# A hyperbolic transformer block on one core: q, k, v kept in PSUM, biases as one-partition products, row scalars of eight tiles

## The chip, the core and the metric

The kernel runs on one core of one Trainium2 chip. The metric is the device time of one execution in microseconds (us); a lower figure is better. Times are medians of several runs on the same chip. Each profile comes from one execution, recorded by the hardware profiler: its span runs from the first instruction to the last, and its own time is a little longer. Engine names: PE is TensorE (matmul), PEld its weight loads, DVE is VectorE, ACT is ScalarE, POOL is GpSimd, SP is SyncE, which issues the DMAs here.

## The reference

The block works on x of 128 x 64 x 256 (8192 tokens of width D = 256, 16 heads of 16) with a condition vector of 256 per sequence. All is in 32-bit floats. Vectors live in the Poincare ball: `logmap0` and `expmap0` go to the tangent space and back and only change a row's length; `mobius_add` is the ball's addition.

```
ada = t_emb @ w_ada + b_ada                     # six vectors of 256 per sequence
xn = layer_norm(logmap0(x))
xm = expmap0(xn * (1 + sc_msa) + sh_msa)
q, k, v = (_to_heads(plin(xm, w, b)) for each)  # plin: expmap0(logmap0(x) @ w + b)
attn = softmax(qt @ kt / sqrt(16)) ; out_h = expmap0(attn @ vt)   # qt, kt, vt = logmap0
x = mobius_add(x, expmap0(g_msa * logmap0(plin(_from_heads(out_h), w_o, b_o))))
xn = layer_norm(logmap0(x)) ; xm = expmap0(xn * (1 + sc_mlp) + sh_mlp)
ff = plin(plin(xm, w_f1, b_f1), w_f2, b_f2)
result = input + mobius_add(x, expmap0(g_mlp * logmap0(ff)))
```

`logmap0(expmap0(u))` is u times a factor: 1, or the largest allowed length over the length of u. Many steps therefore reduce to one clip factor per row, or per row and head.

## The kernel before

**Tiles.** 128 tokens (two sequences of 64) make a tile, 64 in all; two tiles are a pair, four are a quad. A group G is 4 tiles, so there are 16 groups of one quad each. Each group goes through `attention` and then `mlp`.

**Attention of a quad.** `modulated` (line 791) scales and shifts x into y (ACT or DVE), multiplies and adds the condition rows (DVE, POOL), squares (ACT) and finds the clip factor fy per row. `transposed` (809) turns y over on PE into a wide PSUM tile and copies it to yT. Then `attention_pair` (832) runs twice: products with wqkv into a wide PSUM tile qk per tile; one DVE instruction per tile (line 843) forms u = qk * fy + bias in SBUF, which frees the PSUM; ACT squares u; DVE sums the squares per head (hs) and over all heads; a reciprocal root (Ln and Exp on ACT, three steps on DVE) gives the factor g per head; POOL scales q and k in place (859), DVE scales v into ve (861). Then come transposes of q and k (tq), scores (sc, products on 32 x 64 pieces of the array), Exp, products with ve (av, on 64 x 64 pieces), division, transposes (tz), the product with wo and its bias (wp), and `gated` (820), with products and sums of squares. At the group's end `mobius_scalars` (624) works out two scalars per row from these sums in 31 DVE instructions on 128 x 4 or 128 x 8 numbers, and a and b are applied.

**MLP of a quad.** `norm_scalars` (583) gives the layer norm's scalars in 32 DVE instructions on 128 x 4 numbers, then `modulated` and a scaling of y by fy (974), `transposed`, products with two 256 x 256 matrices that were made at the start from w_f1 and w_f2 (hm for the row's length, hw for the value), the clip factor fh, `gated`, `mobius_scalars`, and the output. For the first layer norm the same scalars are computed in a few batches of many tiles (`statistics`).

**Biases.** The q, k, v bias is broadcast over 128 partitions and added by the DVE instruction of line 843. wo's and the MLP's biases are products over 128 partitions with `first`, a matrix whose first row is ones and the rest zeros.

**PSUM.** The eight banks are two wide tiles of two banks (tag `dbl`: qk, tq, two sc at once, av, tp) and four narrow ones of one bank (`bank`: tz, wp, hm, hw and the fillers).

**Order.** The class `Plan` collects all operations with their dependences and an estimated cost each. `run` (150) walks through time: whenever an engine is free it takes the ready operation with the smallest key that finds its buffers free. The key is the group's number; an MLP's key is its group's plus LAG = 3. An operation with several possible engines goes to whichever is free first. A DVE operation that may not run beside POOL is held back. A PE group (`pl.group`) is issued without anything in between. When PE finds nothing, it gets a filler: a 128 x 128 product of the identity (`warm`, 1021). The order found is then issued as it stands, each engine working through its own queue in that order; all DMAs go through SP's queue.

Of the kernel before, what the change touches and what calls it, by code (L numbers as in the profile page):

```python
# [23 lines left out]
SCL = 2.0**-16  # L24
# [31 lines left out]
class Plan:  # L56
# [367 lines left out]
    def mm(self, out, lhsT, rhs, start, stop):  # L424
        n, k = self._n(rhs), lhsT.shape[0]
        occ = 2 * max(n / 1200.0 + 0.002, 0.11) if k == 128 else 0.031 if k == 64 else 0.0356
# [20 lines left out]
def kernel(  # L447
# [44 lines left out]
    G = 4  # L492
    NG = NT // G
    R = _beta(HD / 2, 0.5) / _beta(D / 2, 0.5)
    assert S == 64 and D == 256 and NT % G == 0 and G % 4 == 0
# [19 lines left out]
    def bank(name):  # L515
        return pl.tile(ps, [P, 512], "bank", name, 4, space="psum")

    def dbl(name):
        return pl.tile(ps, [P, 1024], "dbl", name, 2, space="psum")
# [18 lines left out]

    ves = [C([P, 2, H, HD + 1], f"ve{k}") for k in range(2)]
    for v in ves:  # L540
        nc.vector.memset(v, R)
# [7 lines left out]
    def load_x(g):  # L549
        t = T([P, G, D], "x", f"x{g}", 2)  # L550
        for h in range(G // 4):
            i0 = g * G + 4 * h
            pl.dma(t[:, 4 * h : 4 * h + 4, :], x_t[:, i0 : i0 + 4, :], 512 * KB, rows.last if g else None)
        xs[g] = t


    def rsqrt_core(o, ss, tag, room=0):

        shape = list(ss.shape)
        room = [P, max(shape[1], room)] if len(shape) == 2 else shape  # L560
        e = small(room, tag + "e", 2)[:, : shape[1]]
        pl.act(e, ss, AF.Ln)
        pl.act(e, e, AF.Exp, scale=-0.5)
        t = small(room, tag + "t", 2)[:, : shape[1]]
# [4 lines left out]
    def rsqrt_scaled(ss, tag):  # L569

        shape = list(ss.shape)
        m = small(shape, tag + "m", 2)
        pl.ts(m, ss, EPS2, SCL, ALU.max, ALU.mult)
        o = small(shape, tag + "o", 2)
        rsqrt_core(o, m, tag)
        return o

    def clip_factor(o, ss, tag):

        r = rsqrt_scaled(ss, tag)  # L580
        pl.ts(o, r, A * RSCL, 1.0, ALU.mult, ALU.min)

# [41 lines left out]
    def mobius_scalars(x2, wp, xpd, tag):  # L624
# [3 lines left out]
        def sc(k, bufs=1):  # L628
            return small([P, G], tag + k, bufs)

        p2 = wp[:, 1, :]
        r = rsqrt_scaled(wp, tag + "r")
# [41 lines left out]
    for n, w in ((0, 512), (1, 1024)):  # L674
        wada.append([T([P, w], "yTm" if n else "hT", f"wada{n}{c}", 2 if n else NJ + 1) for c in range(2)])
    for n in range(3):
        bada.append(T([P, 512], "hT", f"bada{n}", NJ + 1))
        ada.append(T([P, 512], "hT", f"ada{n}", NJ + 1))
# [8 lines left out]
    bo = C([P, D], "bo")  # L687
# [408 lines left out]
```

## Time and profile before

| | |
|---|---|
| median of 3 runs | 939.68 us (939.16 to 941.25) |
| profiled execution, own time | 937.61 us |
| its span | 935.4 us |
| PE / DVE / ACT / POOL busy | 86% / 87% / 56% / 18% |
| mean granted TensorE clock | 0.931 |
| instructions in the profile | 25226 |
| moved by DMA | 92.07 MB, mean 98 GB/s |

In a row of a group, the names are out<-in, then partitions x elements, the count after x, then busy us in all and the mean duration of one in ns, then the idle time of the engine just before them and what ended it. Buffer names end in a for attention and m for the MLP. A 32-bit product appears as two MATMUL instructions. In a timeline row the first two numbers are start and duration in us. Durations of successive instructions of one engine overlap a little, so a total of durations is more than the engine's occupied time.

### The profile page before, as it was taken

How to read it: one execution, taken by the hardware profiler on the slowest of the kernel's cores; microseconds unless marked ns; L12 is line 12 of the kernel's file. 1: busy time of each engine (PE TensorE's matmuls, PEld its weight loads, DVE VectorE, ACT ScalarE, POOL GpSimd, SP SyncE). 2: the span in 40 equal slices, each digit the busy share in tenths (PEclk: the TensorE clock that was granted, in tenths of full speed). 3: DMA queues.
4: the chain of work that ended last, by engine and by line, in shares of the span. 5: the costliest groups of instructions: out<-in, count | busy, mean ns of one | idle time of the engine just before them, and what ended most of it. 6: DMA issues, size and time to landing. Idle time of an engine off the chain costs nothing.

```text
span 935.4 us, 25226 instructions
## 1 busy us (share of the span) xinstructions
PE 802.7 (86%) x9356; PEld 631.3 (67%) x9356; DVE 817.8 (87%) x3521; ACT 523.4 (56%) x1575; POOL 170.7 (18%) x158
## 2 busy tenths in 40 slices
PE   6989897889888797988879988979898799988786
PEld 4555666758676675867667757858685686667676
DVE  5767979998998999898989998897988889997987
ACT  2342455756565655566557666556555566755542
POOL 0020213112130321202032212121130312221110
PEclk9899888999999899999989998898989799997999
DMA  6793333233332242224225223332232233211222
GB/s 197 232 263 114 109 103 100 80 97 101 114 86 75 77 114 72 75 78 122 81 70 134 92 60 103 90 113 81 80 114 80 58 94 89 80 59 47 68 68 68
DMA packets 77131, 92.07 MB, mean 98 GB/s; under 512 B 7120, under 2 KB 59088, under 8 KB 77008
## 3 DMA queue, kind: packets, MB, share of 16 engines
q1 hardware_dynamic: 77008, 90.47, 33.2%
q8 instruction: 73, 1.20, 0.5%
q14 instruction: 50, 0.41, 0.1%
HBM read 81.27 MB, written 9.18 MB: 97 GB/s over the span
## 4 chain that ended last, share of the span: by engine, by line
DVE 23%; PE 21%; ACT 10%; issue 4%; POOL 1%; DVEq 0%; POOLq 0%; ACTq 0%
PE wpa L427 3%; PE hmm L427 3%; PE ava L427 3%; PE wt L1023 2%; DVE ua L382 2%; PE hwm L427 2%; PE sca L427 2%; DVE hs L395 2%; PE tqa L431 1%; PE qkva L427 1%; DVE bx L382 1%; ACT j2m L420 1%; ACT j2a L420 1%; PE tpm L431 1%; ACT qxa L420 1%
## 5 line engine op out<-in xcount | busy, mean ns | idle before, releaser
L427 PE MATMUL qkva<-wqkv,yTa 128*128 128x512 f32 (+1 forms) x512 | 178.3, 499 | 15.6 <-DVE ua L382 5.3
L427 PEld LDWEIGHTS qkva<-wqkv,yTa 128*128 128x128 f32 x512 | 96.7, 194 | 90.8 <-issue 61.0
L1023 PE MATMUL wt<-ident 128*128 128x128 f32 x828 | 124.8, 305 | 1.8 <-DVE fm L382 1.4
L375 POOL TENSOR_TENSOR ua<-ua,g 128x512 f32<-128x512 f32 x64 | 73.7, 1171 | 281.0 <-DVE g L382 81.0
L1023 PEld LDWEIGHTS wt<-ident 128*128 128x128 f32 x828 | 115.9, 217 | 9.0 <-issue 5.8
L420 ACT ACTIVATE usqa<-ua 128x768 f32<-128x768 f32 x64 | 53.9, 842 | 67.8 <-DVE ua L382 38.7
L375 POOL TENSOR_TENSOR ym<-ym,mdm 128x512 f32<-128x512 f32 x32 | 42.9, 1347 | 214.8 <-DVE rho L382 61.4
L427 PEld LDWEIGHTS ava<-ve,pta 64*64 64x64 f32 x4096 | 70.2, 146 | 13.9 <-ACT pta L420 8.3
L427 PE MATMUL ava<-ve,pta 64*64 64x17 f32 x4096 | 74.5, 215 | 4.5 <-ACT pta L420 4.3
L427 PE MATMUL hmm<-wm,yTm 128*128 128x256 f32 x256 | 70.7, 397 | 5.2 <-ACT yTm L406 3.2
L420 ACT ACTIVATE pta<-sca 128x1024 f32<-128x1024 f32 x64 | 61.9, 1017 | 21.3 <-PE sca L427 21.3
L420 ACT ACTIVATE qxa<-tqa,par 128x512 f32<-128x512 f32 x64 | 43.6, 685 | 49.8 <-PE tqa L431 37.1
L382 DVE SCALAR_TENSOR_TENSOR ua<-qkva,fya,bqkv 128x768 f32<-128x768 f32 x64 | 64.7, 1011 | 7.1 <-PE qkva L427 6.6
L427 PE MATMUL wpa<-wo,zTa 128*128 128x256 f32 x256 | 70.1, 398 | 0.0
L431 PE MATMUL tqa<-ident,ua 128*128 128x128 f32 x256 | 44.6, 320 | 28.9 <-POOL ua L375 28.9
L427 PE MATMUL hwm<-wm,yTm 128*128 128x256 f32 x256 | 66.1, 381 | 0.0
L395 DVE TENSOR_REDUCE hs<-usqa 128x48 f32<-128x768 f32 x64 | 60.6, 947 | 3.7 <-ACT usqa L420 3.6
L427 PE MATMUL sca<-qxa,kTa 32*64 32x128 f32 x2048 | 46.3, 307 | 19.5 <-ACT qxa L420 13.0
L427 PEld LDWEIGHTS hmm<-wm,yTm 128*128 128x128 f32 x256 | 48.0, 196 | 15.9 <-ACT yTm L406 5.7
L375 POOL TENSOR_TENSOR ya<-ya,mda 128x512 f32<-128x512 f32 x30 | 39.9, 1335 | 100.6 <-DVE ya L372 28.5
L431 PEld LDWEIGHTS tqa<-ident,ua 128*128 128x128 f32 x256 | 33.4, 160 | 35.1 <-POOL ua L375 33.7
L427 PEld LDWEIGHTS sca<-qxa,kTa 32*64 32x64 f32 x2048 | 36.2, 147 | 29.7 <-ACT qxa L420 19.1
(257 smaller groups left out, 1808.9 us busy)
## 6 DMA issues: line engine op xcount, KB each, us to landing
mda<-ada_d SPq DMA_DIRECT2D x64, 256.0 KB, 4.1
mdm<-ada_d SPq DMA_DIRECT2D x64, 256.0 KB, 4.0
x<-in_x_dram SPq DMA_DIRECT2D x16, 512.0 KB, 3.7
xr<-in_x_dram SPq DMA_DIRECT2D x32, 256.0 KB, 2.8
gaa<-ada_d SPq DMA_DIRECT2D x64, 128.0 KB, 2.9
gmm<-ada_d SPq DMA_DIRECT2D x64, 128.0 KB, 3.0
out_dram<-p SPq DMA_DIRECT2D x16, 512.0 KB, 3.4
xp<-in_x_dram SPq DMA_DIRECT2D x30, 256.0 KB, 2.8
```

The source lines that it names most:

```text
L375: fn2 = lambda: self.nc.gpsimd.tensor_tensor(out, a, b, op)
L382: fn = lambda: self.nc.vector.scalar_tensor_tensor(out, a, s, b, op0, op1, **({} if accum is None else {"accum_out": accum}))
L395: fn = lambda: self.nc.vector.tensor_reduce(out, a, AX.X, ALU.add)
L420: fn = lambda: self.nc.scalar.activation(out, a, func, scale=scale, **kw)
L427: fn = lambda: self.nc.tensor.matmul(out, lhsT=lhsT, rhs=rhs, start=start, stop=stop)
L431: self.add([("PE", lambda: self.nc.tensor.transpose(out, a, ident), 0.112, 0.2, False)], [a, ident], [out])
L1023: nc.tensor.matmul(wt[:, 0:P], lhsT=ident, rhs=ident, start=True, stop=True)
```

## The change

- **q, k, v in PSUM.** qk is now one wide tile for q and k of both tiles of a pair, and vv one narrow tile for both v. They stay unscaled; squares are taken from PSUM by ACT (1024 and 512 elements at once), the factors are found, and DVE writes u = qk * g and ve = vv * g from PSUM. The row's clip factor f cancels in the factor per head where that clips, and else enters through a lower limit (`lim`, from `rq`), so fy isn't applied to q, k, v. POOL no longer takes part. A constant GC left out of g goes into the scale of the Exp and the constant column of ve.
- **Biases by one-partition products.** Since the rows are not scaled by f, the bias has to be added as bias / f: `clip_factor` also gives inv = 1/f, `transposed` turns it over on PE (four transposes of a broadcast column into a narrow tile) and copies it to rT, and a product of one partition of rT and one of the bias adds it in PSUM. The partitions are 0, 32 and 64 (for the MLP 0, 32, 64 and 96). wo's bias becomes one product of 512 columns per pair.
- **MLP.** y is no longer scaled by fy; the sums and fh are multiplied by it instead. hm and hw of a quad are each one wide PSUM tile.
- **Row scalars of 8 tiles.** The groups are quad 0, then (1, 2), (3, 4) to (13, 14), then 15: nine in all. `mobius_scalars` and the MLP's `norm_scalars` run once per group, on up to 8 columns.
- **PSUM and SBUF.** Three wide tiles and two narrow ones. y has two buffers in place of one, x is loaded in four buffers of a quad, and start-up data shares other tags. LAG is 3.5, the batches of statistics are cut at other quads, and the planner has a cost for one-partition products.

```diff
     def bank(name):
-        return pl.tile(ps, [P, 512], "bank", name, 4, space="psum")
+        return pl.tile(ps, [P, 512], "bank", name, 2, space="psum")
     def dbl(name):
-        return pl.tile(ps, [P, 1024], "dbl", name, 2, space="psum")
+        return pl.tile(ps, [P, 1024], "dbl", name, 3, space="psum")
...
+    GROUPS = [[0]] + [[q, q + 1] for q in range(1, NQ - 1, 2)] + [[NQ - 1]]
...
-    def clip_factor(o, ss, tag):
+    def clip_factor(o, ss, tag, inv=None):
         r = rsqrt_scaled(ss, tag)
         pl.ts(o, r, A * RSCL, 1.0, ALU.mult, ALU.min)
+        if inv is not None:
+            t = small(list(ss.shape), tag + "i")
+            pl.stt(t, ss, RSCL / A, r, ALU.mult, ALU.mult)
+            pl.ts(inv, t, 1.0, None, ALU.max)
...
-    def transposed(y, tag):
+    def transposed(y, inv, tag):
...
+        rT = T([P, 4, P], "rT" + tag[0], f"rT{tag}", 2)
+        rp = bank(f"rp{tag}")
+        with pl.group("PE", [rT]):
+            for t in range(4):
+                pl.tr(rp[:, t * P : (t + 1) * P], inv[:, t : t + 1].to_broadcast([P, P]), ident)
+        pl.copy(rT.rearrange("p t s -> p (t s)"), rp, eng="ACT/DVE")
+        return yT, rT
...
-            pl.stt(u[:, t, :], qk[:, 0 : 3 * D], fy[:, t0 + t : t0 + t + 1], bqkv, ALU.mult, ALU.add)
...
+                for c in range(2):
+                    pl.mm(qk[:, t], yT[:, c, cols], wqkv[:, c, 0:512], c == 0, False)
+                    pl.mm(vv[:, t], yT[:, c, cols], wqkv[:, c, 512:768], c == t == 0, False)
+            for t, o_, r, n0, n1_, stop in (
+                (0, qk, 0, 0, 512, True), (1, qk, 32, 0, 512, True), (0, vv, 64, 512, 768, False), (1, vv, 64, 512, 768, True)
+            ):
+                pl.mm(o_[:, t], rT[r : r + 1, t0 + t, :], bqkv[r : r + 1, n0:n1_], False, stop)
+        pl.act(usq, qk, AF.Square)
+        pl.act(vsq, vv, AF.Square)
+        pl.reduce(hs[:, :, 0:2, :].rearrange("p t a h -> p t (a h)"), usq.rearrange("p t (h e) -> p t h e", e=HD))
+        pl.reduce(hs[:, :, 2, :], vsq.rearrange("p t (h e) -> p t h e", e=HD))
+        pl.reduce(hf.rearrange("p t a -> p (t a)"), hs.rearrange("p t a h -> p (t a) h"))
+        pl.stt(lim, hf, 1.0 / R**2, rq[:, t0 : t0 + 2].unsqueeze(2).to_broadcast([P, 2, 3]), ALU.mult, ALU.max)
+        pl.stt(hsf, hsf, 1.0, lim..., ALU.mult, ALU.max)
+        pl.act(e, hs1, AF.Ln, scale=SCL)
+        pl.act(e, e, AF.Exp, scale=-0.5)
+        pl.stt(hs1, hs1, SCL, e, ALU.mult, ALU.mult)
+        pl.stt(hs1, hs1, -0.5, e, ALU.mult, ALU.mult)
+        pl.stt(g, hs1, 1.5, e, ALU.add, ALU.mult)
...
-            pl.tt(uq, uq, gq.unsqueeze(2).to_broadcast([P, 2 * H, HD]), ALU.mult, eng="POOL")
...
+            pl.tt(u[:, t]..., qk[:, t]..., g4[:, t, 0:2]..., ALU.mult)
+        pl.tt(ve[:, :, :, 0:HD], vv..., g4[:, :, 2]..., ALU.mult)
...
-            for t in range(4):
-                pl.ts(y[:, t, :], y[:, t, :], fy[:, t : t + 1], None, ALU.mult, eng="ACT/DVE")
...
+                        for t in (t0, t0 + 2):
+                            r = 64 * m + 32 * (t // 2)
+                            pl.mm(o_[t], rT[r : r + 1, t, :], bm[r : r + 1, m * D : (m + 1) * D], False, t0 == 1)
...
+            pl.tt(f2, fy, fy, ALU.mult)
+            pl.tt(nh, nh, f2, ALU.mult)
...
+            pl.tt(fh, fh, fy, ALU.mult)
```

311 lines of the change are left out of this document (166 added, 145 removed).

## The prediction

> **What bounds the kernel now.** I read the page first, then the three stretches 0 to 150, 150 to 840 and 840 to 936 us, then groups by shape, then the timeline of single instructions for true spacing.
>
> ```profile
> PE 802.7 (86%) x9356; PEld 631.3 (67%) x9356; DVE 817.8 (87%) x3521; ACT 523.4 (56%) x1575; POOL 170.7 (18%) x158
> L1023 PE MATMUL wt<-ident 128*128 128x128 f32 x828 | 124.8, 305 | 1.8 <-DVE fm L382 1.4
> ```
>
> DVE is the fullest engine. PE looks as full, but 124.8 us of its 802.7 are fillers (wt, line 1023), products that nobody reads, issued only when PE has nothing else: useful PE is 678 us, 72%. ACT and POOL have room.
>
> ```profile
> 150.00:840.00 690.00, 599.58 (x7553) 477.37 (x7552) 625.28 (x2688) 423.10 (x1268) 142.11 (x125) 0.94 0.31 89
> ...
> 150.00:840.00 690.00, 78.07 (x489) 71.34 (x487) 0.94 0.31 89
> ```
>
> These are the windows of all engines (length, then PE, PEld, DVE, ACT, POOL busy) and of line 1023 alone. In the middle 690 us DVE is busy 625.3, or 90.6%, so DVE sets the pace there. Useful PE is 599.6 - 78.1 = 521.5 us, or 75.6%. The middle is my unit: it holds about 13 of 16 quads, a share of 0.81. In the edges loading, setup and the last quads' chains bind more than any engine.
>
> **DVE, pair by pair (32 pairs).** Rows of the groups by shape; the groups between them are left out.
>
> ```profile
> L382 DVE SCALAR_TENSOR_TENSOR ua<-qkva,fya,bqkv 128x768 f32<-128x768 f32 x64 | 64.7, 1011 | 7.1 <-PE qkva L427 6.6
> L395 DVE TENSOR_REDUCE hs<-usqa 128x48 f32<-128x768 f32 x64 | 60.6, 947 | 3.7 <-ACT usqa L420 3.6
> L372 DVE TENSOR_TENSOR ve<-ua,g 128x256 f32<-128x256 f32 x64 | 34.2, 548 | 0.0
> L372 DVE TENSOR_TENSOR za<-ava,rd 128x256 f32<-128x256 f32 x64 | 26.8, 420 | 0.1
> L372 DVE TENSOR_TENSOR x<-wpa,gaa 128x512 f32<-128x512 f32 x32 | 21.9, 686 | 3.2 <-PE wpa L427 3.1
> L382 DVE SCALAR_TENSOR_TENSOR rht<-rht,rhe 128x102 f32<-128x102 f32 x32 | 11.3, 354 | 0.0
> L372 DVE TENSOR_TENSOR rht<-rhe,rhm 128x102 f32<-128x102 f32 x32 | 10.6, 330 | 3.5 <-ACT rhe L420 3.4
> L382 DVE SCALAR_TENSOR_TENSOR rho<-rht,rhe 128x102 f32<-128x102 f32 x32 | 8.2, 257 | 0.0
> L395 DVE TENSOR_REDUCE hs<-hs 128x6 f32<-128x96 f32 x32 | 7.9, 247 | 0.0
> L382 DVE SCALAR_TENSOR_TENSOR g<-rho,lim 128x96 f32<-128x96 f32 x32 | 7.9, 247 | 0.0
> L350 DVE TENSOR_SCALAR lim<-rho 128x6 f32<-128x6 f32 x32 | 7.3, 228 | 0.0
> L350 DVE TENSOR_SCALAR rhm<-hs 128x102 f32<-128x102 f32 x32 | 6.6, 206 | 0.0
> ```
>
> Removed per pair: ua 2 x 1.011, hs 2 x 0.947, ve 2 x 0.548, the small reduction 0.247, and six short ones 0.206 + 0.330 + 0.354 + 0.257 + 0.228 + 0.247 = 1.62. Together 6.88 us. Added: from PSUM, 256 elements take 0.420 (za) and 512 take 0.686 (x<-wpa,gaa), 1.04 ns more an element. So the reduction of 1024 takes 1.22 and that of 512 0.69; the scaling of u, now on DVE, 2 x 0.686; ve in one piece 0.686; then 0.247 + 0.228 + 0.247 + 3 x 0.257 = 1.49 for the short ones. Together 5.46. The gain is 1.42 a pair, but two instructions fewer also lose two overlaps of about 0.08 (below, a 0.16 instruction is followed after 0.07), so 1.26: **-40 us** over 32 pairs. The bias add alone would have gained more; the scaling that moves over from POOL eats 1.37 of it.
>
> **DVE, scalars of 8 tiles.**
>
> ```profile
> 388.01 0.16 DVE L372 TENSOR_TENSOR n2c<-n2z,n2l 128x4 f32<-128x4 f32 x1
> 388.21 0.16 DVE L372 TENSOR_TENSOR n2q<-n2c 128x4 f32<-128x4 f32 x1
> ...
> 411.28 0.16 DVE L382 SCALAR_TENSOR_TENSOR mmk<-mmk,mmm 128x4 f32<-128x4 f32 x1
> 411.35 0.16 DVE L382 SCALAR_TENSOR_TENSOR mak<-mak,mam 128x4 f32<-128x4 f32 x1
> ```
>
> By the code norm_scalars issues 32 DVE instructions and mobius_scalars 31, twice: 94 a group. Groups fall from 16 to 9, so 7 x 94 = 658 instructions vanish; eight columns in place of four add next to nothing (the 102-wide row above takes only 0.1 more). One costs 0.07 where chains interleave (411.28 to 411.35) and 0.20 where a chain runs alone (388.01 to 388.21): 46 to 132 us. I take 0.115, nearer the dense end since this stream mostly has other work between: **-76 us**.
>
> **DVE, the rest.** Scaling of the MLP's y by fy goes (28 on DVE, 12.0 us by the first row below; some 9 by spacing); added are eight short instructions a quad (two for inv in the attention and two in the MLP, rq, f2, nh, fh), 8 x 16 x 0.115 = 15, and about a third of 32 copies of rT at 0.6: 7. Net +13.
>
> ```profile
> L350 DVE TENSOR_SCALAR ym<-ym,fym 128x256 f32<-128x256 f32 x28 | 12.0, 440 | 0.1
> L375 POOL TENSOR_TENSOR ua<-ua,g 128x512 f32<-128x512 f32 x64 | 73.7, 1171 | 281.0 <-DVE g L382 81.0 <-DVE mak L382 38.7 <-DVE mam L372 30.0
> L372 DVE TENSOR_TENSOR ve<-ua,g x64: 406/418/1284, 37.3 to 838.9; 128x256 f32<-128x256 f32 x64
> ```
>
> The last row (min, median, max) shows DVE held up beside POOL: 0.418 as a rule, 1.284 at worst, longer by most of a POOL instruction. Without POOL's 73.7 us other DVE rows lose some of such holds: from 0 to 20 us, I take -10. The sum is -40 - 76 + 13 - 10 = -113: DVE falls from 818 to about **705 us**, with bounds 650 to 750.
>
> **PE gets what DVE loses in part.**
>
> ```profile
> 401.85 7.90 PE L427 MATMUL qkva<-wqkv,yTa 128*128 128x512 f32 x24
> ...
> 385.03 1.21 PE L427 MATMUL sca<-qxa,kTa 32*64 32x128 f32 x64
> ```
>
> The first row is three tiles, 12 instructions of 512 and 12 of 256 columns: 9216 columns in 7.90, so 0.44 us for 512 and 0.22 for 256, two instructions to a product. The new q, k, v bias is two products of 512 and two of 256: 2.64 us a pair if one after the other. They read partitions 0, 32 and 64, and small tiles can overlap: the second row puts 64 instructions of 128 columns, 0.11 each alone and 7.0 in all, into 1.21. If the three places ran wholly side by side the longest would take 0.88. Neither is shown for one-row products, so I take the middle, 1.76: +56 (28 to 84). The MLP's 8 biases of 256 columns a quad take 3.52 now; in pairs at two places they take 1.76 to 3.52, middle 2.64: -14 (-28 to 0). wo's bias keeps its columns: 0.
>
> ```profile
> 381.48 1.04 PE L431 MATMUL tpm<-ident,ym 128*128 128x128 f32 x8
> ...
> 383.21 0.59 PE L427 MATMUL wpa<-bo,first 128*128 128x256 f32 x2
> 383.65 1.03 PE L427 MATMUL wpa<-wo,zTa 128*128 128x256 f32 x4
> 384.51 0.59 PE L427 MATMUL wpa<-bo,first 128*128 128x256 f32 x2
> 385.03 1.21 PE L427 MATMUL sca<-qxa,kTa 32*64 32x128 f32 x64
> 386.17 1.13 PE L427 MATMUL hmm<-wm,yTm 128*128 128x256 f32 x4
> 387.14 0.59 PE L427 MATMUL hmm<-bm,first 128*128 128x256 f32 x2
> ```
>
> Eight transposes take 1.04; eight more a quad for rT: +17. Going to the small tile and back costs: wo's bias to its successor 0.44 within the tile form (383.21 to 383.65), 0.52 into sca; four hmm after sca 0.97, against 0.86 for four wo (383.65 to 384.51): 0.19 there and back. One trip a pair and four a quad in the MLP, 96 in all: +18. The Trainium skill (TensorEngine Tiling (Array Packing), Key Properties) says that changing the tiling mode drains TensorE, and its page TensorE: Matmul & The Clock Gate, Part 2, puts a drain at about 128 cycles. By these, as an estimate, a switch costs 0.05 and the trips 10 us; the trace agrees in kind and is dearer.
>
> PE: 56 - 14 + 17 + 18 = +77, so useful PE is **755 us**, bounds 695 to 800. PE becomes the fuller engine, and the fillers shrink.
>
> **ACT** trades 2 squares of 768 for one of 1024 and one of 512, loses its part of y times fy and half its short Ln and Exp, gains rT copies: about even, at half load. **DMA** gains one 128 KB load; statistics of quads 1 and 2 come in one batch, so four early xp loads go ahead of quad 1 where two did. That lies in the first 100 us and I price it at 0, covered by setup products; 3 us without cover.
>
> **A new wait.** The q, k, v group now waits for 1/f to be computed, transposed and copied (before, only the later bias add needed f). Behind it on PE stands every later product in the written order. It is hidden while the previous quad's pairs occupy PE (y has two buffers now). Without that cover it costs five short steps of 0.2, Ln and Exp, transposes and copy, some 2.6 us a quad.
>
> **The sum.** In the middle, PE 521.5 + 0.81 x 77 = 584 and DVE 625.3 - 0.81 x 113 = 534. If PE fills as DVE does today (90.6%), the middle takes 584 / 0.906 = 645 us, 45 less, with DVE at 83%. The edges give 5 of DVE's 21 us there, being mostly chains. Span 935.4 - 50 = 885; own time 2.2 above its span (937.61), and the runs' median 939.68 another 2.1: **889**, of which I call 888.
>
> **Rivals.**
> (a) The one-row products overlap wholly, like sca. Then PE gains only 77 - 28 - 14 = 35: middle 521.5 + 28 = 550, / 0.906 = 607, 83 less, and with the edges **852**. For it: sca's row. Against: its neighbours alternate over eight places, whereas here both instructions of a product share one.
> (b) PE doesn't fill like DVE, since its groups are long and need free PSUM. At PE's present 86.9% with fillers (599.6 / 690) the middle takes 672 and the run **917**. Serial one-row products (PE +119, middle 618 / 0.906 = 682) give 927.
> (c) Slower: PSUM. qk and vv stay through squares, reductions, Ln, Exp and scaling, some 7 us by the durations above with DVE never late, where the bias add freed qk after one instruction of 1.0. Three wide tiles serve qk, tq, two sc at once, av, the transposes, and now hm and hw, which also wait for a factor; vv takes one of only two narrow ones. sc cannot start while two of three are held. From 1.6 us of added PE wait a pair (50 / 32) the gain is gone; at 2.1 the run is at **956**. Against: by durations and waits as I count them (an estimate) a quad holds wide tiles for qk 23, sc 12, hw 10, av 7, tq 6, hm 6 and tp 5 us, some 70 of 3 x 55.
> (d) The planner puts things in an order that gains nothing: 938 to 941.
>
> **How the numbers follow.** Forecast (870 to 905) 0.44; (a) 0.20; (b) 0.23; (c) 0.10; (d) 0.03. A measurement of this kernel tells 0.2%, about 2 us, from no change. Faster 0.87, same 0.03, slower 0.10. The range goes from 850, (a), to 936, past both forms of (b), and leaves out (c), (d) and little of (a).
>
> **What would show it.** DVE near 705 and useful PE near 755 with fillers well under 125; bias rows of about 1.76 us a pair in the timeline; no ua on POOL; ma, mm and n2 rows with x9; PE's share above DVE's in the middle. Wrong if DVE stays fullest, if PE waits for DVE u rows (PSUM held), or if q, k, v products wait for the rT copy.

## The result, and the profile after

The changed kernel takes **914.0 us** (median; 910.88 to 921.11) against 939.54 us for the kernel before on the same chip: ratio 0.9735, 95% interval 0.9678 to 0.9793. It is faster by 25.5 us where 51.5 us (939.54 - 888) were forecast. The profiled execution is its slowest: own time 921.11, span 919.3 us, mean granted clock 0.905 (before: 0.931).

The page of the changed kernel, busy time of each engine and the fillers:

```profile
PE 814.0 (89%) x9236; PEld 577.4 (63%) x9236; DVE 724.2 (79%) x2923; ACT 501.6 (55%) x1480; POOL 97.1 (11%) x91
...
L1084 PE MATMUL wt<-ident 128*128 128x128 f32 x388 | 68.4, 322 | 5.0 <-ACT j1a L420 3.2
```

Useful PE is 814.0 - 68.4 = 745.6 us (forecast 755). DVE is 724.2 (forecast 705). PE is now the fuller engine, as forecast. So the work came out about as predicted; the time did not.

To see where the time lies I cut both executions at equal shares of the work: where PE had done 15% and 90% of its useful time. Before, that is at 138 and 814 us; after, at 155 and 789. First the kernel before, then the changed one: windows of all engines (length; PE, PEld, DVE, ACT, POOL busy; then granted clock, DMA share, GB/s), then of the fillers alone.

```profile
138.00:814.00 676.00, 587.16 (x7151) 468.18 (x7150) 612.02 (x2634) 415.02 (x1251) 139.59 (x123) 0.94 0.31 90
814.00:935.40 121.40, 96.62 (x1026) 82.28 (x1026) 103.58 (x492) 56.50 (x185) 14.86 (x14) 0.91 0.21 62
...
138.00:814.00 676.00, 78.61 (x494) 72.56 (x494) 0.94 0.31 90
814.00:935.40 121.40, 28.06 (x202) 26.35 (x202) 0.91 0.21 62
```

```profile
155.00:789.00 634.00, 569.90 (x7071) 405.10 (x7070) 511.59 (x1987) 384.16 (x1111) 72.23 (x62) 0.90 0.31 87
789.00:919.30 130.30, 113.72 (x964) 87.90 (x962) 104.56 (x495) 56.06 (x198) 11.85 (x12) 0.94 0.25 72
...
155.00:789.00 634.00, 9.65 (x30) 6.07 (x30) 0.90 0.31 87
789.00:919.30 130.30, 39.33 (x254) 35.13 (x254) 0.94 0.25 72
```

The same three quarters of the work take 676 us before and 634 after: 42 less, where the forecast had 45. But the start is 17 us longer (138 to 155) and the end 9 us longer (121.4 to 130.3). Useful PE fills (569.90 - 9.65) / 634 = 88.4% of the middle; before, it was (587.16 - 78.61) / 676 = 75.2%. (This execution is 7 us over the median, so 7 of these microseconds are not in the time that is compared.)

The granted clock moved too: in the middle it was 0.94 before and is 0.90 after. The four executions of the changed kernel, which issue the same instructions in the same order, took 921.11 us at a clock of 0.905, 914.05 at 0.911, 913.95 at 0.913 and 910.88 at 0.918: some 8 us for each hundredth.

The prediction's own stretch of 150 to 840 us, in the changed kernel, all engines and fillers:

```profile
150.00:840.00 690.00, 623.15 (x7787) 444.98 (x7781) 556.73 (x2230) 414.00 (x1212) 75.76 (x68) 0.91 0.29 83
...
150.00:840.00 690.00, 21.50 (x103) 15.97 (x103) 0.91 0.29 83
```

Useful PE fills (623.15 - 21.50) / 690 = 87.2% of it, and DVE 80.7%.

The one-partition products, in the timeline of PE of the changed kernel (start, duration, engine, line, what):

```profile
419.60 0.70 PE L432 MATMUL qka<-bqkv,rTa 1*128 1x512 f32 x2
419.62 0.69 PE L432 MATMUL vva<-bqkv,rTa 1*128 1x256 f32 x2
420.14 0.59 PE L432 MATMUL qka<-bqkv,rTa 1*128 1x512 f32 x2
420.15 0.59 PE L432 MATMUL vva<-bqkv,rTa 1*128 1x256 f32 x2
420.67 0.66 PE L436 MATMUL tza<-ident,za 128*128 128x128 f32 x4
```

The whole bias of a pair takes 420.67 - 419.60 = 1.07 us with the trip to the small tile, where the forecast had 1.76 + 0.19. 1.07 - 0.19 is the 0.88 that rival (a) gave for places that run wholly side by side. The MLP's behave alike:

```profile
398.39 0.70 PE L432 MATMUL hmm<-bm,rTm 1*128 1x256 f32 x4
399.02 1.35 PE L432 MATMUL hmm<-wm,yTm 128*128 128x256 f32 x5
```

Two products take 0.63, so a quad's eight take 2.52 with their trips; they took 3.52.

Groups by shape of the changed kernel, PE first (busy us, mean ns | idle before):

```profile
L432 PE MATMUL qka<-wqkv,yTa 128*128 128x512 f32 x256 | 144.6, 648 | 3.0 <-DVE maden L372 2.2 <-ACT qxa L420 0.8
...
L436 PE MATMUL tqa<-ident,ua 128*128 128x128 f32 x256 | 44.1, 326 | 27.5 <-DVE ua L372 22.5 <-ACT pta L420 3.6 <-DVE mmk L372 1.5
...
L436 PE MATMUL rpa<-ident,fia 128*128 128x128 f32 x64 | 13.5, 349 | 2.4 <-DVE fia L350 1.9 <-ACT j1a L420 0.4
L436 PE MATMUL rpm<-ident,fim 128*128 128x128 f32 x64 | 10.0, 279 | 5.4 <-ACT j1a L420 4.0 <-DVE n2sv L382 1.5
```

The first two groups had these rows in the kernel before:

```profile
L427 PE MATMUL qkva<-wqkv,yTa 128*128 128x512 f32 x256 | 125.8, 615 | 15.6 <-DVE ua L382 5.3 <-ACT pta L420 4.9 <-ACT yTa L406 4.6
...
L431 PE MATMUL tqa<-ident,ua 128*128 128x128 f32 x256 | 44.6, 320 | 28.9 <-POOL ua L375 28.9
```

Now the rows of DVE in the changed kernel:

```profile
L372 DVE TENSOR_TENSOR ua<-qka,g 128x512 f32<-128x512 f32 x64 | 42.4, 682 | 0.3
L395 DVE TENSOR_REDUCE hs<-usqa 128x64 f32<-128x1024 f32 x32 | 38.7, 1209 | 10.2 <-ACT usqa L420 10.1
L372 DVE TENSOR_TENSOR ve<-vva,g 128x512 f32<-128x512 f32 x32 | 21.7, 679 | 0.0
L395 DVE TENSOR_REDUCE hs<-vsqa 128x32 f32<-128x512 f32 x32 | 21.6, 675 | 0.0
L404 DVE COPY zTa<-tza 128x256 f32<-128x256 f32 x32 | 12.7, 419 | 38.9 <-PE tza L436 35.0 <-ACT zTa L406 3.9
```

The DVE durations are those forecast: 682 for a scaling of 512 (686), 1209 for the reduction of 1024 (1220). But all 32 copies zTa now go to DVE (11 did before), and DVE stands 35 us waiting for PE before them.

### The profile page after: what moved, and what is told of

Read it like the earlier page. It is cut to its first block, busy times and chain, and to the rows that moved or that the text cites. A ratio compares the mean times of both kernels' runs of the same rounds, so it can differ in the third digit from the quotient of the medians.

```text
span 919.3 us, 24167 instructions
## 1 busy us (share of the span) xinstructions
PE 814.0 (89%) x9236; PEld 577.4 (63%) x9236; DVE 724.2 (79%) x2923; ACT 501.6 (55%) x1480; POOL 97.1 (11%) x91
## 4 chain that ended last, share of the span: by engine, by line
PE 42%; DVE 29%; ACT 13%; issue 9%; DMA 5%; POOL 1%; SPq 1%; DVEq 0%; POOLq 0%; ACTq 0%
PE hmm L432 8%; PE ava L432 6%; PE wpa L432 5%; PE qka L432 5%; PE hwm L432 5%; PE tqa L436 3%; PE vva L432 3%; PE sca L432 2%; DVE bx L382 2%; DVE hs L395 2%; DVE p L382 2%; DVE ua L372 2%; PE wt L1084 1%; PE tza L436 1%; DMA mdm<-ada_d 1%
## 5 line engine op out<-in xcount | busy, mean ns | idle before, releaser
L432 PE MATMUL qka<-wqkv,yTa 128*128 128x512 f32 x256 | 144.6, 648 | 3.0 <-DVE maden L372 2.2
L432 PEld LDWEIGHTS vva<-wqkv,yTa 128*128 128x128 f32 x256 | 51.5, 203 | 72.9 <-issue 62.6
L432 PEld LDWEIGHTS ava<-ve,pta 64*64 64x64 f32 x4096 | 75.9, 157 | 18.4 <-issue 6.0
L432 PE MATMUL vva<-wqkv,yTa 128*128 128x256 f32 x256 | 81.0, 400 | 3.0 <-DVE n1st L410 1.5
L1084 PE MATMUL wt<-ident 128*128 128x128 f32 x388 | 68.4, 322 | 5.0 <-ACT j1a L420 3.2
L420 ACT ACTIVATE usqa<-qka 128x1024 f32<-128x1024 f32 x32 | 32.4, 1014 | 67.2 <-PE vva L432 59.2
L436 PE MATMUL tqa<-ident,ua 128*128 128x128 f32 x256 | 44.1, 326 | 27.5 <-DVE ua L372 22.5
L1084 PEld LDWEIGHTS wt<-ident 128*128 128x128 f32 x388 | 57.2, 204 | 17.3 <-PE wt L1084 8.8
L432 PEld LDWEIGHTS qka<-wqkv,yTa 128*128 128x128 f32 x256 | 50.6, 208 | 13.0 <-issue 4.1
L432 PEld LDWEIGHTS wpa<-wo,zTa 128*128 128x128 f32 x256 | 47.5, 196 | 15.9 <-ACT zTa L406 5.9
L432 PEld LDWEIGHTS hwm<-wm,yTm 128*128 128x128 f32 x256 | 46.2, 189 | 13.5 <-issue 8.4
```

Of the source, the lines that this page charges most:

```text
L420: fn = lambda: self.nc.scalar.activation(out, a, func, scale=scale, **kw)
L432: fn = lambda: self.nc.tensor.matmul(out, lhsT=lhsT, rhs=rhs, start=start, stop=stop)
L436: self.add([("PE", lambda: self.nc.tensor.transpose(out, a, ident), 0.112, 0.2, False)], [a, ident], [out])
L1084: nc.tensor.matmul(wt[:, 0:P], lhsT=ident, rhs=ident, start=True, stop=True)
```

## The experiments

Each kernel was run beside the kernel before on its own chip (that median lay between 939.9 and 941.8 us), so ratios are compared. "The earlier pair" means `attention_pair` as in the kernel before, put into the changed kernel with everything else left: q, k, v go to SBUF in one DVE instruction with f and bias, POOL scales q and k. Seven of the 18 results (`samerow`, `fill0`, `b_lag35`, `oldpair`, `oldboth_single`, `op_psum24`, `op_bufs`) lie more than 2 us outside every range expected for them, so the sizes of the effects were poorly foreseen.

**First round: four single causes.** `single`: groups of one quad throughout.

```diff
-    GROUPS = [[0]] + [[q, q + 1] for q in range(1, NQ - 1, 2)] + [[NQ - 1]]
+    GROUPS = [[q] for q in range(NQ)]
```

> The changed kernel with every quad a group of its own, so the row scalars run on 4 columns 16 times again; all else as changed. Theory A (PE now sets the pace, so what DVE saves is worth nothing): 914 us plus or minus 8, although DVE gets about 70 us more busy time (724 to about 790). Theory B (the cut of DVE's short instructions carries the gain): about 950, since 658 instructions at 0.115 us come back. If below 908, the groups of two quads themselves cost time at start and tail.

899.41 us, ratio 0.9549 (0.9481 to 0.9617). One-quad groups are faster than the change's own by 15 us, although DVE has 47 us more to do (771.5 busy). This is not the price of the scalars of eight tiles themselves: `ends`, below, keeps them in the middle and is 12 us faster still.

`nobias`: the products that add the q, k, v bias are left out; the order is kept.

```diff
-                    pl.mm(qk[:, t], yT[:, c, cols], wqkv[:, c, 0:512], c == 0, False)
+                    pl.mm(qk[:, t], yT[:, c, cols], wqkv[:, c, 0:512], c == 0, c == 1)
...
-                pl.mm(o_[:, t], rT[r : r + 1, t0 + t, :], bqkv[r : r + 1, n0:n1_], False, stop)
+                pl.mm(o_[:, t], rT[r : r + 1, t0 + t, :], bqkv[r : r + 1, n0:n1_], False, stop, leave=True)
```

> The changed kernel without the four one-partition products of each pair (the q, k, v bias is left out of the result), the order of everything else kept as it is. In its trace these took about 1.07 us a pair, 34 us in all. Theory A (PE sets the pace in nearly all of the run): 25 to 34 us less, 880 to 889. Theory C (PE, DVE and ACT wait on one another in turn, an order that does not fit the real durations): under half of it, 898 to 912.

898.71 us, 0.9533 (0.9467 to 0.9599), useful PE 777.6 - 68.1 = 709.5. So 36 us of PE work are worth 15 us of time, 0.4 us each.

`cost`: the planner's cost of a one-partition product is lowered, for the pair to the measured one.

```diff
-            occ = 0.0356 if n < 256 else n / 800.0
+            occ = 0.0356 if n < 256 else n / 1440.0
```

> The changed kernel, its planner told that a one-partition product of n columns costs n / 1440 us (1.07 us a pair, as its trace shows) instead of n / 800 (1.92 a pair); every instruction is the same, only the written order moves. Theory A: little to gain from order, 905 to 918. Theory C (the gain was lost since the order was written for a slower PE than the real one): 865 to 895.

896.05 us, 0.9533 (0.9441 to 0.9626). The instructions are the same; only the order differs. The planner had charged 1.92 us a pair for products that take 1.07. But the edit touches the MLP's products as well: it takes a quad's eight from 2.56 to 1.42 us, where the trace has 2.52. So the costs as a whole did not come nearer to the measured ones, and the 18 us show what another order of the same instructions is worth, not that a truer cost gave it.

`ends`: two-quad groups only from quad 3 to 12.

```diff
-    GROUPS = [[0]] + [[q, q + 1] for q in range(1, NQ - 1, 2)] + [[NQ - 1]]
+    GROUPS = [[q] for q in range(3)] + [[q, q + 1] for q in range(3, 13, 2)] + [[q] for q in range(13, NQ)]
...
-    batches = {0: (1, 3), 1: (3, 5), 3: (5, 10), 7: (10, 16)}
+    batches = {0: (1, 2), 1: (2, 5), 3: (5, 10), 7: (10, 16)}
```

> The changed kernel with groups of one quad for quads 0 to 2 and 13 to 15, two quads only between them, and the first layer norm's statistics of quad 1 apart from those of quad 2. Theory D (the first 15% and last 10% of PE's work, which stand 17 and about 20 us worse than before in the trace, are late because groups of two quads hold the MLPs back): 880 to 895. If the ends are late for another reason (the slower granted clock, the wait for rT): 908 to 918.

887.64 us, 0.9414 (0.9352 to 0.9476): 26 us from the groups (and one batch of statistics) at the two ends, with DVE busy 732.6. This is the size of the loss that the windows show there (17 + 9), but most of the gain does not lie there. The same cut, at 15% and 90% of PE's useful time:

```profile
0.00:150.00 150.00, 126.78 (x1088) 80.91 (x1088) 102.19 (x430) 59.52 (x162) 12.24 (x15) 0.93 0.60 172
150.00:763.00 613.00, 550.64 (x7348) 388.27 (x7350) 524.99 (x2144) 384.51 (x1131) 75.85 (x67) 0.94 0.33 92
763.00:884.60 121.60, 105.11 (x770) 81.69 (x764) 105.44 (x544) 54.92 (x204) 10.56 (x10) 0.92 0.27 81
```

Start 150, middle 613 and end 121.6, against 155, 634 and 130.3: of some 35 us of span 21 are gained in the middle and 14 at the two ends, and the granted clock is 0.937 against 0.905.

**Second round: do these add, and what do the products cost when they can't overlap?** `ends_cost` has both of the last two edits.

> Both mendings at once: groups of one quad at both ends and the planner's cost of one-partition products at n / 1440. If late ends (27 us in the run ends) and the order written for too slow a PE (18 us in the run cost) are two separate losses: 868 to 874. If both mend the same waits: 880 to 890.

867.41 us, 0.9202 (0.9156 to 0.9249). The two edits add: 26 + 18 = 44 expected of single effects, 47 measured. So they hardly mend the same waits. Its page:

```profile
PE 777.1 (90%) x9230; PEld 552.5 (64%) x9230; DVE 724.8 (84%) x3123; ACT 495.0 (57%) x1488; POOL 96.6 (11%) x91
```

DVE's busy time is that of the changed kernel (724.2), in 53 us less span: DVE waits less and works as much. PE's useful time, though, falls from 745.6 to 777.1 - 61.3 = 715.8 us with the same products, at a granted clock of 0.951 against 0.905.

`samerow`: all four products of the bias use partition 0.

```diff
-                (0, qk, 0, 0, 512, True), (1, qk, 32, 0, 512, True), (0, vv, 64, 512, 768, False), (1, vv, 64, 512, 768, True)
+                (0, qk, 0, 0, 512, True), (1, qk, 0, 0, 512, True), (0, vv, 0, 512, 768, False), (1, vv, 0, 512, 768, True)
```

> The changed kernel with all four one-partition products of a pair on partition 0 in place of 0, 32 and 64, order kept. Theory overlap (they ran side by side since their places in the array differ): 2.6 to 2.8 us a pair in the trace in place of 1.07, 50 to 56 us more PE work; by the run without these products, where 34 us of PE work were worth 15, that is 22 to 26 us, 935 to 942. If one place overlaps as well: 914 plus or minus 8.

960.07 us, 1.0182 (1.0125 to 1.0240). Its PE timeline, the bias of one pair:

```profile
455.71 1.98 PE L432 MATMUL qka<-bqkv,rTa 1*128 1x512 f32 x4
457.53 1.16 PE L432 MATMUL vva<-bqkv,rTa 1*128 1x256 f32 x4
458.62 1.16 PE L432 MATMUL sca<-qxa,kTa 32*64 32x128 f32 x32
```

458.62 - 455.71 = 2.91 us where three places take 1.07. Times 32 pairs this is 59 us of PE, and the run is 46 us longer: 0.8 us for each us of PE, where taking the products away gave 0.4. Without the overlap the change would have been slower than the kernel before.

`fill0`: no fillers after the planner's 60th microsecond.

```diff
-                    if e == "PE" and self.fill[0] < now < self.fill[1] and live[tag] < bufs:
+                    if e == "PE" and 60.0 > now > self.fill[0] and live[tag] < bufs:
```

> The changed kernel without fillers after the planner's 60th us. Theory clock (fewer fillers in the changed kernel let the granted clock fall from 0.931 to 0.905 to 0.918, and PE's own products stretch by some 20 us): the granted clock falls further, to 0.85 to 0.89, and the time rises to 920 to 940. If the clock follows the useful products alone: 910 to 918 at about 0.90.

898.30 us, 0.9535 (0.9498 to 0.9571), clock 0.899. With no fillers after the start the clock falls only from 0.905 to 0.899, and the run is 16 us *faster*: the order is another one. So some 15 us hang on which order comes out; a difference of that size between two orders does not show its cause by itself, and that holds for `single` and `cost` as well.

`oldpair_single`: the earlier pair, and groups of one quad.

```diff
-    GROUPS = [[0]] + [[q, q + 1] for q in range(1, NQ - 1, 2)] + [[NQ - 1]]
+    GROUPS = [[q] for q in range(NQ)]
...
+            pl.stt(u[:, t, :], qk[:, 0 : 3 * D], fy[:, t0 + t : t0 + t + 1], bqkv, ALU.mult, ALU.add)
...
+            pl.tt(uq, uq, gq.unsqueeze(2).to_broadcast([P, 2 * H, HD]), ALU.mult, eng="POOL")
...
-                attention_pair(i0 + 2 * pr, 2 * pr, yT, rT, rq, x_q, x1, wp[:, 0, c], wp[:, 1, c], xpd[:, c])
+                attention_pair(i0 + 2 * pr, 2 * pr, yT, fy, x_q, x1, wp[:, 0, c], wp[:, 1, c], xpd[:, c])
```

> The run single (899 us) with the attention of a pair as it was before: bias and factor added by one DVE instruction from PSUM, scaling of q and k on POOL, no rT in the attention; MLP, buffers, three wide and two narrow PSUM tiles and LAG 3.5 as changed. Theory P (q, k, v in PSUM carry the gain): DVE is again at 815 or more and sets the pace, 930 to 942. Theory Q (the gain comes from the MLP, the buffers and the key, and q, k, v in PSUM only move work from DVE to PE): 885 to 905.

891.63 us, 0.9458 (0.9419 to 0.9498). This kernel has neither of the two headline parts (q, k, v in PSUM; scalars of eight tiles), and yet gains 50 us, twice what the change gains. What is left in it are the buffers in SBUF, the PSUM split, LAG, the MLP's part, and smaller edits (wo's bias in one product, the batches of statistics, start-up data).

**Third round: which of these, and the two headline parts in a fair order.** `single_cost` joins two edits shown; `oldpair_ends` is the earlier pair in the groups of `ends`; `b_lag35` is the kernel before with one line changed; `ends_cost_fill0` joins three edits.

> The run single (899 us) with the planner's cost of one-partition products at n / 1440, so that q, k, v in PSUM are judged in an order written for what they really take. Theory Q (they only move work from DVE to PE): 885 to 900, no better than the attention as before in the same frame (oldpair_single, 891.6). Theory R (they are worth something, and only the wrong cost hid it): 870 to 882.

892.02 us, 0.9464 (0.9424 to 0.9504): with the cost at n / 1440, worth 7 us here, q, k, v in PSUM stand level with the earlier pair (0.9458) when groups are one quad.

> The run oldpair_single (891.6 us, DVE 773 us busy, 87% of its span) with groups of two quads for quads 3 to 12. DVE sets the pace there, so the theory that row scalars of 8 tiles pay where DVE is the bound says 5 x 94 instructions fewer at 0.115 us, 54 us of DVE less, over 0.87: at most 62 us, and PE or waits take over before that: 845 to 872. If groups of two quads pay nowhere: 884 to 900.

854.77 us, 0.9091 (0.9048 to 0.9134): with the earlier pair, and two-quad groups in the middle, 37 us better than one-quad groups. Scalars of eight tiles do pay; and q, k, v in PSUM are 13 us behind (867.41).

```diff
-    LAG = 3
+    LAG = 3.5
```

> The kernel before with LAG = 3.5 in place of 3 and nothing else. Theory L (the later key of the MLP carries most of the 48 us between the kernel before and oldpair_single): 895 to 918. Theory M (the MLP's unscaled y, the wide hm and hw, and the second y buffer carry it): 932 to 942.

950.64 us, 1.0097 (1.0063 to 1.0132). LAG alone makes the kernel before 1% slower, not faster; by itself it does not bring the 50 us.

> The run ends_cost (867.4 us) without fillers after the planner's 60th us. In the changed kernel leaving them out was worth 15.7 us at a granted clock no lower than 0.899. If fillers get in the way of useful products and PSUM: 850 to 862. If that gain was the luck of another order: 863 to 875, with a granted clock below ends_cost's 0.951.

876.77 us, 0.9281 (0.9221 to 0.9341), clock 0.911 against 0.951. In this order leaving out the fillers costs some 9 us (the two intervals just meet) together with a lower clock; in the former order it gained 16.

**Fourth round: the change with the earlier pair and nothing else.** `oldpair` is `oldpair_single` with the change's own groups.

> The changed kernel with only the attention of a pair as it was before (bias and factor by one DVE instruction, scaling of q and k on POOL); groups of two quads, MLP, buffers and PSUM tiles as changed. Theory Q (q, k, v in PSUM with one-partition biases cost time here, since they move work to PE, which sets the pace): 865 to 895, well below 914. If they carry the gain of 25 us: 930 to 942. If they are worth nothing either way: 910 to 918.

**848.77 us**, 0.9020 (0.8977 to 0.9062). Its page:

```profile
PE 767.3 (90%) x9074; PEld 554.4 (65%) x9074; DVE 738.3 (87%) x2905; ACT 506.2 (60%) x1499; POOL 170.3 (20%) x154
...
L1066 PE MATMUL wt<-ident 128*128 128x128 f32 x546 | 96.5, 317 | 6.3 <-ACT j1a L420 2.9 <-DVE rTm L404 0.5
```

In the change's own groups and order, putting q, k, v in PSUM (848.77 to 914.0) costs **65 us**. It adds 745.6 - (767.3 - 96.5) = 75 us to PE and takes 738.3 - 724.2 = 14 from DVE. As an estimate, 29 of the 75 are the lower clock: 745.6 x 0.905 / 0.941 = 717, 46 more than `oldpair`. In other frames the same swap costs far less: 8 us with one-quad groups (899.41 - 891.63), nothing there with the cost at n / 1440, and 13 us with `ends` and that cost (867.41 - 854.77; the runs with the earlier pair keep the old cost). So most of the 65 us goes with the same losses that `ends_cost` takes away, 47 us. The four kernels with the change's own planner form a square:

| ratio to before | groups of one quad | groups of two quads |
|---|---|---|
| earlier pair | 0.9458 | 0.9020 |
| q, k, v in PSUM | 0.9549 | 0.9735 |

Two-quad groups take 4 to 5 points off with the earlier pair and put 2 on with q, k, v in PSUM. That is not against the scalars of eight tiles: in the middle alone such groups pay with q, k, v in PSUM too, 899.41 to 887.64 (`single` to `ends`) and 892.02 to 867.41 (`single_cost` to `ends_cost`).

`oldboth_single` undoes the MLP's part as well:

```diff
-            yT, rT = transposed(y, inv, tag)
+            for t in range(4):
+                pl.ts(y[:, t, :], y[:, t, :], fy[:, t : t + 1], None, ALU.mult, eng="ACT/DVE")
+            yT = transposed(y, None, tag)
...
-                            pl.mm(o_[t], rT[r : r + 1, t, :], bm[r : r + 1, m * D : (m + 1) * D], False, t0 == 1)
+                            pl.mm(o_[t], first, bm[:, m * D : (m + 1) * D], False, t0 == 1)
```

> The run oldpair_single (891.6 us) with the MLP's products as before too: y scaled by fy, biases over 128 partitions; what remains of the change are three wide and two narrow PSUM tiles with wide hm and hw, the second buffer of y, other buffers, and LAG 3.5. Theory M1 (the MLP's unscaled y carries the 48 us): 930 to 942. Theory M2 (buffers and PSUM tiles carry it): 888 to 902, with DVE 9 us busier and PE some 20 us busier than oldpair_single.

877.60 us, 0.9332 (0.9277 to 0.9388): with the MLP's products and y scaling as before as well, 14 us better than `oldpair_single`. The MLP's part brings nothing here; with two-quad groups the same step is worth 4 us, with intervals that overlap (`oldboth`, below).

`op_psum24` takes `oldpair_single` back to the PSUM split of the kernel before:

```diff
-        return pl.tile(ps, [P, 512], "bank", name, 2, space="psum")
+        return pl.tile(ps, [P, 512], "bank", name, 4, space="psum")
...
-        return pl.tile(ps, [P, 1024], "dbl", name, 3, space="psum")
+        return pl.tile(ps, [P, 1024], "dbl", name, 2, space="psum")
```

> The run oldpair_single (891.6 us) with two wide and four narrow PSUM tiles as before, hm and hw still wide. Theory W (the third wide tile is what lets PE and DVE run ahead of each other): 915 to 942. Theory Y (the second y buffer and the other SBUF buffers carry the gain): 888 to 900.

882.84 us, 0.9364 (0.9324 to 0.9404): two wide and four narrow PSUM tiles, as before, do no worse with the earlier pair. How the changed kernel itself would run with this split wasn't tried.

**Fifth round: the buffers, and both parts undone.** In `op_bufs`, x has 2 buffers, x1 3, p2 2 and y 1, as in the kernel before, with the rest as in `oldpair_single`; in `op_x` only x has 2.

```diff
         xs[q] = T([P, 4, D], "x", f"x{q}", 4)
+        pl.byname[xs[q].tensor.name].bufs = 2
...
             x1 = T([P, 4, D], "x1", f"x1_{qd}", 6)
+            pl.byname[x1.tensor.name].bufs = 3
...
```

> The run oldpair_single (891.6 us) with as many SBUF buffers in use as before: x two, x1 three, p2 two, y one. Theory Z (the 48 us between the kernel before and oldpair_single come from more SBUF buffers, so that a later quad can start while an earlier one still holds its rows): 925 to 950. If neither buffers nor PSUM tiles nor the MLP's products carry it: 885 to 900.

973.20 us, 1.0339 (1.0260 to 1.0417). In this frame the SBUF buffers carry 973.2 - 891.6 = **82 us**. The figure can't be carried over to the kernel before: that has the same counts and is 31 us faster than this run, with LAG 3, and with start-up data that did not share x1's and p2's buffers. The kernel before with the larger buffers was not tried. At the cut of 15% and 90%, 58 of the 84 us between the profiled spans lie in the middle (683 against 625 us); the granted clock is 0.894 against 0.934. Its page:

```profile
PE 826.1 (85%) x9222; PEld 601.2 (62%) x9222; DVE 820.7 (84%) x3594; ACT 509.8 (52%) x1538; POOL 170.3 (18%) x154
```

and that of `oldpair_single`, which has the larger buffers:

```profile
PE 788.5 (89%) x9126; PEld 562.3 (63%) x9126; DVE 773.3 (87%) x3576; ACT 511.1 (57%) x1554; POOL 170.6 (19%) x156
```

With nearly as many DVE instructions (3594 and 3576) DVE is busy 47 us less. No row of the pages says which wait for a buffer this is. What I argue from the code, and haven't shown, is that with two buffers of x the first step of a later quad waits for the rows that an earlier quad's last step still reads, so fewer quads are open at a time, and a short chain on DVE has less to run between its steps.

> The run oldpair_single (891.6 us) with two buffers for x as before in place of four; y, x1 and p2 keep theirs. If x is the buffer that mattered (attention's last step still reads it, so with two buffers the third quad's first step waits for the first quad's last): 915 to 945. If y or x1: 888 to 900.

926.56 us, 0.9817 (0.9736 to 0.9898): x's buffers alone are 35 of the 82 us. How the other 47 divide among x1, p2 and y wasn't tried.

> The run oldpair (848.8 us: attention of a pair as before, groups of two quads, more buffers) with the MLP's y scaled and its biases over 128 partitions as before too, so of the change only buffers, tiles, key and row scalars of 8 tiles are left. Among groups of one quad this step was worth 14 us (891.6 to 877.6): 833 to 842 if it holds here; 849 plus or minus 6 if that was the luck of an order; above 855 if the MLP's part helps once DVE has less to do.

**844.82 us**, 0.8970 (0.8905 to 0.9035), the lowest time of all, though its interval overlaps that of `oldpair`: buffers, groups, PSUM split and LAG of the change, pair and MLP products of the kernel before.

```profile
PE 761.6 (90%) x9030; PEld 577.0 (68%) x9030; DVE 727.8 (86%) x2846; ACT 511.5 (61%) x1520; POOL 170.7 (20%) x160
```

Its DVE is as busy as the changed kernel's (727.8 and 724.2) without any of the work that was moved to PE.

**Where the start loses.** One part of the 65 us can be followed in the traces: the first pair of quad 0. In each, PE's timeline of the changed kernel and then of `oldpair`:

```profile
46.90 1.09 PE L436 MATMUL tqa<-ident,ua 128*128 128x128 f32 x8
...
66.47 13.90 PE L432 MATMUL wmp<-wt 128*128 128x512 f32 x32
...
90.76 0.60 PE L436 MATMUL tza<-ident,za 128*128 128x128 f32 x4
...
99.17 1.02 PE L432 MATMUL qka<-wqkv,yTa 128*128 128x512 f32 x2
```

```profile
39.86 0.38 PE L436 MATMUL tqa<-ident,ua 128*128 128x128 f32 x2
...
49.93 1.43 PE L436 MATMUL tza<-ident,za 128*128 128x128 f32 x4 [1.49 <-DVE za L372]
...
65.24 13.90 PE L432 MATMUL wmp<-wt 128*128 128x512 f32 x32
...
90.91 9.62 PE L432 MATMUL qkva<-wqkv,yTa 128*128 128x512 f32 x28
```

The first transposes of q and k come 7 us later (46.90 against 39.86). PE is not idle just before them, so no wait for the factor shows there; they stand later in its order. In the changed kernel's timeline the first pair's group starts 4 us later (27.55 against 23.48), behind the transposes for rT; then come the products with wada (35.28 to 40.26, against 31.27 to 34.70), and in both kernels the second pair's group, with its bias 40.26 to 46.90, against 34.70 to 39.86. The transposes of z, which run ahead of the setup products (wmp) in `oldpair`, come behind them (90.76 against 49.93), and quad 1 starts 8 us later (99.17 against 90.91).

## Why the prediction was wrong, point by point

- **Called right: who gets the work.** DVE 724 (bounds 650 to 750), useful PE 746 (695 to 800), PE above DVE, no ua on POOL, fillers well under 125. The middle gained 42 (forecast 45), though by two errors that cancel: the sum on PE was 9 smaller, and the fill 88.4% in place of 90.6%. That PE came out within 9 us is luck too, as the points on the clock and on the one-row products show.
- **The step that failed: "The edges give 5 of DVE's 21 us there".** They lost 26: 138 + 121.4 us before, 155 + 130.3 after. Of the 34 us between the forecast's span (885) and the profiled one (919.3) this is 31 (7 of the 34 belong to this execution alone). The prediction priced the statistics' batches there at 0 and called the rest of the edges chains, without following the first and last groups one by one. The cause of the loss stays open in part: the first pair's later place in PE's order is seen in the start, but `ends`, which takes the two-quad groups away from both ends, gains only 14 of its 35 us of span there.
- **A term that the sum put at nothing: the granted clock.** It takes PE's work as if the clock stayed. The kernel before ran at 0.931, the changed one at 0.905 to 0.918. Useful PE time multiplied by the clock is nearly the same in kernels with the same products: 745.6 x 0.905 = 675 here, 677 in `ends`, 679 in `cost` and 681 in `ends_cost`, whose clocks go up to 0.951; 631 in the kernel before and 631 in `oldpair`. So PE's time went as one over the clock, and the change's own new work is some 44 us at full clock, not 68. By 8 us a hundredth, the step from 0.931 to the median of 0.912 is, as an estimate, 15 of the 26 us by which 888 was missed. This overlaps with the loss at the edges and does not add to it. Why the clock is lower is not shown.
- **One-row products: rival (a) was right on the mechanism.** They do run side by side: 1.07 a pair with the trip, not 1.95; 34 us in all, not 56 plus a trip a pair. But (a)'s 852 didn't follow. With 34 for the bias, -16 for the MLP's (2.52 - 3.52, in 16 quads) and 13.5 + 10.0 for rT, PE would have had 678 + 42 = 720; it had 746. The other 26 are the old products taking longer: the q and k product has 648 ns a row where the kernel before has 615, at a granted clock of 0.905 against 0.931. By the clock alone, as an estimate, 678 x 0.931 / 0.905 = 697, that is 19 of the 26. In the Trainium skill (TensorE: Matmul & The Clock Gate, Part 3) products in different row groups overlap; the trace agrees, for one-row 32-bit products too, and `samerow` shows the other side.
- **Rival (b) met the time by luck: 917 against 914.** Its reason, that PE would not fill as DVE did, holds: it gave 86.9%, and the stretch from 150 to 840 shows 87.2%. But that stretch now holds 601.65 / 745.6 = 81% of the work, where it held 77%; cut by work the fill is 88.4%, and the rest of the miss lies at the edges. PSUM hold, the cause that (b) and (c) name, is neither shown nor excluded: PE waited 22.5 us for DVE's ua ahead of tq, the sign that the prediction gave for it, but before it waited 28.9 for POOL's ua in the same place; and the split of PSUM was tried with the earlier pair only, where two wide tiles did no worse.
- **Scalars of eight tiles were mis-sized by half: -76 forecast.** From `oldpair_single` to `oldpair` 671 instructions go and DVE loses 773.3 - 738.3 = 35 us, 0.052 each; from `single` to the change 669 go and 47 us, 0.071 each. These are net of copies that changed engine. The price taken was 0.115 with bounds 0.07 to 0.20, so the runs lie at or under the dense end, where chains interleave; that more buffers bring this about is argued only.
- **The pairs were mis-sized as well: -40, and -10 for POOL's holds.** q, k, v in PSUM took 14 us from DVE where 50, less some 9 for the attention's share of short steps and rT copies, were forecast. The rows of the pair are as forecast. Flexible copies took a part of the place (zTa 15 on DVE in `oldpair`, 32 in the change, 7 us more); the rest was not traced.
- **What the prediction left out: the buffers.** Half of what DVE lost came from where no term stood: 818 to 773 without either headline part, and by `op_bufs` (821) that is the buffers. The list of changes has x's and y's, not x1's six for three and p2's four for two. Worth 82 us in the frame of `oldpair_single`, they are more than the whole forecast gain. The changed kernel is faster than the one before although q, k, v in PSUM, in its groups and order, cost it 65 us, which the forecast had priced as a gain.
- **The rival on the other side (slower) was misplaced.** The change does hold something that costs more than it brings: it moves 75 us onto PE (46 at equal clock, by the estimate above) for 14 off DVE. Whether the wide tiles have a part in that was not tried. The rival "the planner puts things in an order that gains nothing", given 0.03, did not come true at 914, but order and grouping are worth more than that chance suggests: cost and ends together are 47 us.

**What stays open.** Why groups of two quads at the ends cost 26 us with q, k, v in PSUM and nothing with the earlier pair (0.9020 with them, 0.9091 without) isn't settled: the start's rows show a delay of 8 us, and kernels with one-quad groups at the ends have that delay too (the first pair's row j3a starts at 98.9 us in `ends`, 97.2 in the change, 59.2 in `oldpair`). Orders differ by some 15 us with no cause that a run separates. What part of the differences between kernels is the granted clock is open as well: `ends_cost` ran at 0.947 to 0.955 where the change ran at 0.905 to 0.918, which by 8 us a hundredth would be some 30 of the 47 us, but `fill0` was faster than the change at 0.888 to 0.899. No run holds the clock fixed. Which buffer wait carries the 82 us is argued only.

## What to carry to other kernels

Price every line of a diff, buffer counts first: a count that lets another quad open can be worth more than the arithmetic that the change is about. Work moved off the fullest engine pays only until the one that takes it is the bound; count what is added there (75 us) against what is saved (14 us). Compare the granted clock of two kernels before reading their busy times against each other. Where an order is written ahead from estimated costs, try more than one: here two orders of the same products differ by 16 to 18 us. And price the first and last groups by themselves.

## What the runs showed of the hardware

One-row 32-bit products at partitions 0, 32 and 64 ran side by side: 1.07 us for two of 512 and two of 256 columns with the change of tile, against 2.91 us when all stand at partition 0. Less the 0.19 us of the change of tile, that is the 0.88 us of the longest place alone; the forecast had taken the middle, 1.76.

Leaving out the fillers lowered the mean granted clock by 0.006 in one order (0.905 to 0.899) and by 0.040 in another (0.951 to 0.911), and the time moved by -16 and +9 us: in the first the new order outweighed the clock, in the second the two are not separated.

PE's useful busy time went as one over the granted clock. Its product with the clock lies between 665 and 682 us in the eight kernels that have all the products of the changed one, in one order or another (clocks 0.899 to 0.951), and between 626 and 641 in the six that have those of `oldpair` (0.894 to 0.951).

The same short DVE instructions cost 0.05 to 0.07 us apiece when some 670 of them are taken out of a kernel with the larger buffers, though each lasts 0.16 in the timeline of the kernel before.
